# Statistics of two context columns in one VectorE instruction, in a fused decoder kernel

## The chip, the core and the metric

The kernel runs on one core of a Trainium2 chip. The core has TensorE (PE, matmuls; its weight loads are listed apart as PEld), VectorE (DVE), ScalarE (ACT) and GpSimd (POOL), and a queue for data movement, SyncE (SP). Each engine takes its own instructions strictly in their written order and waits, where it must, for semaphores that other engines or transfers raise. The metric is the device time of one execution in microseconds (us).

## The reference, cut to what matters

The input x has 8 sequences of 256 tokens and 1024 features; a second input, ctx, has the same shape. Three blocks follow each other, each added to its own input:

```python
x = x + attn(layernorm(x))                 # 4 layers: recurrence over time, then a 128-512-128 feed-forward
x = x + xattn(layernorm(x), ctx)           # the mask comes from ctx
x = x + ffn(layernorm(x))                  # 8 experts, the best 2 for each token
```

The change concerns the second block. For each sequence and each of the 1024 features (there called L), it takes the 256 tokens (there called channels, C) and keeps the `k = 154` with the largest ctx value:

```python
_, topk_idx = jax.lax.top_k(cm, k)                 # k = 154 of 256
mask = zeros.at[b_idx, l_idx, topk_idx].set(1.0)
crucial_features    = mask * x
subcrucial_features = (1 - mask) * x
# maxima and means of both over the channels -> a 7-tap filter -> two gates per feature
return crucial_features * A_S1 + subcrucial_features * A_S2
```

## The kernel before, in words

*Layout.* Features lie on the 128 partitions. ctx is read as 64 columns, one for each of 8 sequences and 8 groups of 128 features; a column is a 128 x 256 tile whose 256 channels lie side by side in fp32. The columns are worked in `PARTS = 4` batches of `GH = 16`; a batch is one tile `ctx` of 128 x 16 x 256, with two buffers.

*The mask without sorting.* `search(hb)` (L200 to L282) is a generator that handles one batch and yields between its parts. It looks for a threshold in each column:

- The guess (L214 to L228): `bn_stats` of each column, then the spread `sd` (L219, and a power of one half on POOL, L220), then the first trial `trial` (L224) and two ends of a bracket around it (L225, L226).
- Four rounds (L229 to L249): ACT counts with 16 `Sign` instructions with an accumulator (L233) how many channels lie above the trial. DVE compares the counts (L236, L237), moves the ends (L239) and forms the next trial (L243 to L248). ACT's next round needs that trial.
- The tail (L250 to L277): three DVE instructions for each column (L255, L257, L258) find the last few values; L281 then writes the mask. `fails` notes a column whose search didn't end; if any did not, a slow search runs (L717 on).

`bn_stats` on a row of values gives six numbers: count, mean and sum of squared deviations of the values at even places, then the same three of those at odd places. The guess uses only two: the even mean (index 1, L224) and the even sum of squares (index 2, L219).

*What stands around it.* While the four searches go, the kernel runs the first block: 16 cells (4 layers x 4 chunks of 512 tokens). A cell is `recurrence` (L586 to L597: scale to y, two multiplications by the turn table, four scans, all on DVE), `second_norm` (L602 to L611) and `feedforward` (L618 to L626); each normalisation goes over PE (L574), DVE (`ve`, L351), POOL (a power, L352) and PE again (L166). Then come `put_out` (L630 on), `normed_x1` (L325) and `kept_and_dropped` (L315, L318), which sums x under the mask of the same chunk. `advance` mixes the searches' parts between the cells. After that the gates, the routing and the experts' matmuls follow (L1098).

*The start.* `load_rows(c)` (L382 to L393) loads 2 MB of x by rows and takes their statistics on DVE (L387, L388). All four loads use **one** buffer, so the load of rows(c+1) waits for the statistics of rows(c). On SP's queue the transfers stand in this order: win, rows(0), x(0), ctx of batch one, w1, w2, rows(1), x(1), half of x(2), rows(2), the other half of x(2), ctx of batch two, rows(3), x(3), then 18 stores of zeros (L412), wo (L653), and the ctx of batches three and four, which wait for a free ctx buffer. `start(c)` projects x(c) to h (L536, L541). The table `turn` is built in a chain of dependent DVE instructions (L439 to L442 for layer 0). The weights are prepared in between: b2f (L556), PE's 16 small matmuls L561 from w1, b1f (L563) from their result, and the scalings L549, L550, L552 and L565.

*What sets the order.* The kernel isn't written in the order in which it runs. A planner (the Tile framework) takes the program, estimates for each instruction when it could start, and lays down one fixed order for each engine; it also puts in the semaphore waits. So an edit in one place can change the order elsewhere.

Of the kernel before, what the change touches and what calls it, by code (L numbers as in the profile page):

```python
# [13 lines left out]
ALU = mybir.AluOpType  # L14
# [3 lines left out]
B, S, D = 8, 256, 1024  # L18
# [24 lines left out]
TINY = 1e-30  # L43
# [3 lines left out]
GH = B * NK // PARTS  # L47
TRIALS = 5
SHARE = -0.2563
# [18 lines left out]
def decoder_kernel(ctx: ExitStack, tc: tile.TileContext, x_t, x_rows, ctx_t, vecs, win_t, w1_t, w2_t, wout_t,  # L68
# [106 lines left out]
    with ExitStack() as early:  # L175
# [6 lines left out]
        v = nc.vector  # L182
# [11 lines left out]
        def load_ctx(hb):  # L194
            ctx_h = tkp.tile([P, GH, S], F32, tag="ctx", name="ctx", bufs=2)
            for q in range(GH // 4):
                b, g = divmod(hb * (GH // 4) + q, 2)
                nc.sync.dma_start(out=ctx_h[:, 4 * q : 4 * q + 4, :].rearrange("p j c -> p (j c)"),
                                  in_=ctx_t[b, g])
            return ctx_h  # L200
# [3 lines left out]
        def search(hb):  # L204

            ctx_h = ctxs[hb] if hb < len(ctxs) else load_ctx(hb)
            def small(name, n=1, dt=F32):
                shape = [P, GH] if n == 1 else [P, GH, n]
                return tkp.tile(shape, dt, tag=f"tk_{name}", name=f"tk_{name}", bufs=2)

            def pair(name, dt=F32):
                return tkp.tile([P, 2, GH], dt, tag=f"tk_{name}", name=f"tk_{name}", bufs=2)

            st = small("st", 6)  # L214
            for i in range(GH):
                v.bn_stats(st[:, i, :], ctx_h[:, i, :])

            sd = small("sd")
            v.tensor_scalar(sd, st[:, :, 2], 2.0 / S, TINY, ALU.mult, ALU.add)  # L219
            nc.gpsimd.tensor_tensor(sd, sd, power, ALU.pow)  # L220

            trial = pair("trial")
            ends = tkp.tile([P, 2, 2, GH], F32, tag="tk_ends", name="tk_ends", bufs=2)
            v.scalar_tensor_tensor(trial[:, 0], sd, -SHARE, st[:, :, 1], ALU.mult, ALU.subtract)  # L224
            v.scalar_tensor_tensor(ends[:, 0, 0], sd, REACH, trial[:, 0], ALU.mult, ALU.add)  # L225
            v.scalar_tensor_tensor(ends[:, 0, 1], sd, -REACH, trial[:, 0], ALU.mult, ALU.add)  # L226
            nc.gpsimd.memset(ends[:, 1, 0], signs(DROP - REACH * SLOPE))
# [2 lines left out]
            for n in range(TRIALS - 1):  # L230
# [16 lines left out]
                trial = pair("trial")  # L247
                v.tensor_tensor(trial[:, 0], ends[:, 0, 0], w, ALU.subtract)  # L248
                yield  # L249
            t, up, m8 = small("t"), small("up"), small("m8", 8)  # L250
# [32 lines left out]


        waiting = [search(hb) for hb in range(PARTS)]
        going = []
        steps = 0
# [40 lines left out]
        with ExitStack() as dec:  # L328
# [9 lines left out]
            h = [wp.tile([P, CT], F32, tag=f"h{c}", name=f"h{c}") for c in range(NCH)]  # L338
# [80 lines left out]
            v = nc.vector  # L419
# [297 lines left out]
    with tc.If(wrong != 0):  # L717
        with tc.tile_pool(name="slow", bufs=2) as tkp:
            for b in range(B):
                for g in range(2):  # L720
# [3 lines left out]
                    t = tkp.tile([P, 4, S], F32, tag="tk", name="tk")  # L724
# [43 lines left out]
    with tc.tile_pool(name="xattn", bufs=2) as cp:  # L768
# [60 lines left out]
        sd = cp.tile([P, 1], F32, name="bn_sd", bufs=1)  # L829
# [278 lines left out]
    v = nc.vector  # L1108
# [179 lines left out]
```

## Time and profile before

| | |
|---|---|
| Time, median of 3 runs | 1188.22 us (1187.46 to 1188.44) |
| The profiled execution, its own time | 1187.67 us |
| Its span, first to last instruction | 1185.9 us |
| Busy in the span: PE / PEld / DVE / ACT / POOL | 995.7 / 490.5 / 579.8 / 476.3 / 261.8 us |
| `bn_stats` of the search (L216) | 64 of 411 ns, 23.1 us |
| `bn_stats` of the rows (L387) | 32 of 666 ns, 20.3 us |
| `Sign` of the search (L233) with its read of the accumulator | 256 of 504 + 189 ns |
| Last masked sum on DVE (L315) ends | 489.2 us |
| Experts' matmuls (L1098) | 1152 of 597 ns |

The profile is of one execution. A line of the timeline gives the start, the duration, the engine, the line of the kernel, the operation, output <- inputs with their shapes, how many in a row, and in brackets how long the engine stood idle before it and what ended that wait. Busy time on an engine isn't time on the path: instructions on one engine overlap a little, and an engine that waits for another costs only if its lateness is passed on. All line numbers here and below are those of the kernel before; in the changed kernel the lines from L231 on stand 6 further down.

### The profile page before, as it was taken

The page shows a single profiled execution, that of the slowest core. Times are in us where ns is not written, and L with a number is a line of the kernel's source. Part 1 is how long each engine was busy: PE and PEld are TensorE (multiplying, and loading weights), DVE is VectorE, ACT ScalarE, POOL GpSimd, SP SyncE. Part 2 cuts the span into 40 slices and gives each one's busy share as a digit, 9 for nine tenths or more (in the row PEclk, how much of TensorE's full clock was granted, in tenths as well). Part 3 has the DMA queues.
Part 4 walks back from the last instruction along what each step waited for, and adds up shares of the span by engine and source line. Part 5 has one row for each costly group of instructions (what it writes and reads, how often), then busy time and mean ns, then how long its engine had stood idle before and what let it go on. Part 6 is the DMA issues. An engine that isn't in the chain of part 4 may idle for free. (4 is left out here: it accounts for less than half of the span.)

```text
span 1185.9 us, 10180 instructions
## 1 busy us (share of the span) xinstructions
PE 995.7 (84%) x2954; PEld 490.5 (41%) x2954; DVE 579.8 (49%) x1783; ACT 476.3 (40%) x1167; POOL 261.8 (22%) x275
## 2 busy tenths in 40 slices
PE   4848878878888687168849999999999999999994
PEld 2414434434444344033424444444444444444442
DVE  8588888868957978787872111111111111111110
ACT  0577667677764567496311211111111111111110
POOL 1111112121111001104476311113213223131111
PEclk8768889989989877578859999999999999999998
DMA  9594010010000000026637854545557477574622
GB/s 386 203 380 168 0 72 1 15 56 1 1 1 1 0 1 1 13 77 227 210 94 240 264 166 116 156 125 123 161 146 231 119 212 212 138 228 96 177 35 37
DMA packets 53840, 144.99 MB, mean 122 GB/s; under 512 B 5232, under 2 KB 14448, under 8 KB 51984
## 3 DMA queue, kind: packets, MB, share of 16 engines
q0 software_dynamic: 17728, 59.88, 20.3%
q1 hardware_dynamic: 35472, 83.97, 19.6%
q8 instruction: 25, 0.41, 0.1%
q10 hardware_dynamic: 576, 0.41, 0.1%
q14 instruction: 39, 0.32, 0.1%
HBM read 106.61 MB, written 37.64 MB: 122 GB/s over the span
## 5 line engine op out<-in xcount | busy, mean ns | idle before, releaser
L1098 PE MATMUL ps_mm<-w_x,xT 128*128 128x512 f32 x1152 | 505.7, 597 | 2.9 <-ACT xT L1092 0.6
L1098 PEld LDWEIGHTS ps_mm<-w_x,xT 128*128 128x128 f32 x1152 | 216.7, 191 | 270.5 <-issue 259.4
L1101 DVE SCALAR_TENSOR_TENSOR y<-ps_mm,held,y 128x512 f32<-128x512 f32 x56 | 42.0, 751 | 358.6 <-PE ps_mm L1098 358.6
L233 ACT ACTIVATE tkj<-ctx,tk_trial 128x256 f32<-128x256 f32 x256 | 129.1, 504 | 40.8 <-DVE tk_trial L248 22.7
L1084 ACT ACTIVATE y<-src,held 128x1024 f32<-128x1024 f32 x28 | 32.1, 1147 | 195.5 <-DMA out_dram<-y,to 160.2
L1092 ACT COPY xT<-ps_tp 128x512 f32<-128x512 f32 x37 | 21.7, 586 | 189.6 <-PE ps_tp L1090 177.5
L352 POOL TENSOR_TENSOR rs<-ve,minus_half 128x4 f32<-128x4 f32 x36 | 41.1, 1142 | 246.5 <-DVE ve L351 224.2
L618 PE MATMUL ps_tp<-z,w 128*128 128x512 f32 x128 | 69.5, 648 | 13.9 <-DVE z L611 12.9
L1102 POOL DMA_INDIRECT out_dram<-y,to x28 | 44.6, 1592 | 159.2 <-DVE y L1101 117.3
L166 PE MATMUL ps_st<-ident,rs 128*128 128x128 f32 x160 | 29.6, 320 | 57.7 <-POOL rs L352 49.2
L1071 POOL DMA_INDIRECT src<-x_rows,to x28 | 29.0, 1035 | 165.3 <-ACT y L1084 164.1
L1101 DVE SCALAR_TENSOR_TENSOR y<-ps_mm,got,y 128x512 f32<-128x512 f32 x18 | 13.5, 750 | 102.7 <-PE ps_mm L1098 96.0
L318 ACT ACTIVATE comb<-comb 128x256 f32<-128x256 f32 x128 | 51.5, 403 | 27.9 <-DVE smax L315 26.2
L624 PE MATMUL ps_mm<-f,w 128*128 128x512 f32 x128 | 61.7, 602 | 0.0
L166 PEld LDWEIGHTS ps_st<-ident,rs 128*128 128x128 f32 x160 | 20.5, 159 | 83.7 <-POOL rs L352 73.5
L1090 PE MATMUL ps_tp<-ident,xn 128*128 128x128 f32 x296 | 39.9, 278 | 16.4 <-ACT xn L1082 16.4
L621 ACT ACTIVATE f<-ps_tp,b1f 128x512 f32<-128x512 f32 x64 | 43.5, 682 | 23.4 <-PE ps_tp L618 23.1
L1090 PEld LDWEIGHTS ps_tp<-ident,xn 128*128 128x128 f32 x296 | 35.4, 144 | 35.9 <-issue 19.0
L574 PEld LDWEIGHTS ps_cols<-mean_w,sq 128*128 128x128 f32 x288 | 39.5, 202 | 22.8 <-ACT sq L571 11.3
L233 ACT ACTIVATION_READ_ACCUMULATOR tkj<-ctx,tk_trial 128x1 f32 x256 | 48.3, 189 | 0.0
L604 PE MATMUL ps_mm<-mi,turned_w 128*128 128x512 f32 x64 | 38.2, 705 | 8.0 <-DVE mi L597 8.0
L536 PE MATMUL ps_tp<-x,win 128*128 128x512 f32 x64 | 37.1, 735 | 5.9 <-DMA x<-in_x_t_dram 2.8
(371 smaller groups left out, 1434.1 us busy)
## 6 DMA issues: line engine op xcount, KB each, us to landing
w_x<-in_expert_w_dram SPq DMA_DIRECT2D x36, 1024.0 KB, 8.4
out_dram<-zero SPq DMA_DIRECT2D x17, 512.0 KB, 7.7
rows<-in_x_rows_dram SPq DMA_DIRECT2D x4, 2048.0 KB, 8.6
x<-in_x_t_dram SPq DMA_DIRECT2D x8, 1024.0 KB, 12.8
ctx<-in_ctx_t_dram SPq DMA_DIRECT2D x16, 512.0 KB, 9.1
x_rows<-row SPq DMA_DIRECT2D x16, 512.0 KB, 2.8
w<-in_w_t_dram SPq DMA_DIRECT2D x2, 1024.0 KB, 11.6
win<-in_win_t_dram SPq DMA_DIRECT2D x1, 512.0 KB, 3.7
```

Source lines behind the costliest of these rows:

```text
L166: nc.tensor.transpose(rb[:, q * P : (q + 1) * P], rs[:, q : q + 1].to_broadcast([P, P]), ident)
L233: nc.scalar.activation(junk, ctx_h[:, i, :], AF.Sign, bias=trial[:, 0, i : i + 1], accum_out=trial[:, 1, i : i + 1])
L318: nc.scalar.activation(comb[:, st, :], comb[:, st, :], AF.Copy, accum_out=ssum[:, st, b, k : k + 1])
L352: nc.gpsimd.tensor_tensor(out_, ve, root, ALU.pow)
L574: nc.tensor.matmul(out=st[:, q : q + 1], lhsT=sq[:, q * P : (q + 1) * P], rhs=mean_w, start=True, stop=True)
L618: nc.tensor.matmul(out=fps, lhsT=w1[:, l, f * P : (f + 1) * P], rhs=z, start=True, stop=True)
L621: nc.scalar.activation(ft, fps, AF.Silu, bias=b1[:, 4 * l + f : 4 * l + f + 1])
L624: nc.tensor.matmul(out=xc, lhsT=w2[:, l, f, :], rhs=ft, start=False, stop=(f == DFF // P - 1), skip_group_check=True)
L1090: nc.tensor.transpose(tp[:, k * P : (k + 1) * P], xn[:, kk * P : (kk + 1) * P], ident)
L1098: nc.tensor.matmul(out=op, lhsT=xT[:, k * P : (k + 1) * P], rhs=ws[k][g], start=(k == 0), stop=(k == NK - 1))
L1101: nc.vector.scalar_tensor_tensor(y[:, o], op, weight, y[:, o], ALU.mult, ALU.add)
L1102: added = nc.gpsimd.indirect_dma_start(out=out[0:ROWS_THEN, :] if apart else out, out_offset=bass.IndirectOffsetOnAxis(ap=token, axis=0), ...
```

## The change

One `bn_stats` now reads two columns at once. Its input is the even channels of both, and goes through them in turn: channel 0 of the first column, channel 0 of the second, channel 2 of the first, and so on, 256 values. The values at even places are then the first column's even channels, those at odd places the second column's. The six numbers of an instruction are thus count, mean and sum of squares of two columns, and fill the first six of the twelve places of a pair in `st`. The reads of `st` are changed to find them there, and `sd` and `trial` are seen in pairs for that; their values are those of the kernel before. There are 8 such instructions for a batch instead of 16.

```diff
@@ -212,16 +212,22 @@
             st = small("st", 6)
-            for i in range(GH):
-                v.bn_stats(st[:, i, :], ctx_h[:, i, :])
+            for i in range(0, GH, 2):
+
+                v.bn_stats(st[:, i : i + 2, :].rearrange("p c f -> p (c f)")[:, 0:6],
+                           ctx_h[:, i : i + 2, ::2].rearrange("p c s -> p s c"))
+            st = st.rearrange("p (h c) f -> p h (c f)", c=2)[:, :, 0:6].rearrange("p h (c f) -> p h c f", c=2)
+            def halves(t):
+                return t.rearrange("p (h c) -> p h c", c=2)
 
             sd = small("sd")
-            v.tensor_scalar(sd, st[:, :, 2], 2.0 / S, TINY, ALU.mult, ALU.add)
+            v.tensor_scalar(halves(sd), st[:, :, :, 2], 2.0 / S, TINY, ALU.mult, ALU.add)
             nc.gpsimd.tensor_tensor(sd, sd, power, ALU.pow)
 
             trial = pair("trial")
             ends = tkp.tile([P, 2, 2, GH], F32, tag="tk_ends", name="tk_ends", bufs=2)
-            v.scalar_tensor_tensor(trial[:, 0], sd, -SHARE, st[:, :, 1], ALU.mult, ALU.subtract)
+            v.scalar_tensor_tensor(halves(trial[:, 0]), halves(sd), -SHARE, st[:, :, :, 1], ALU.mult,
+                                   ALU.subtract)
```

## The prediction

> **What bounds the kernel now.** I began with the page: its chain of waits covers only the last 1.4% of the span (the last expert's matmuls), so it can't price this change. The stages come from the busy time in stretches (columns after the stretch: its length, busy time of PE, PE's weight loads, DVE, ACT and POOL with instruction counts, granted TensorE clock, DMA share, GB/s).
>
> ```profile
> 0.00:80.00 80.00, 42.30 (x117) 24.77 (x118) 58.28 (x250) 33.24 (x106) 15.16 (x41) 0.77 0.80 316
> 80.00:260.00 180.00, 146.74 (x487) 75.26 (x485) 153.71 (x466) 128.02 (x355) 28.79 (x26) 0.88 0.20 71
> 260.00:425.00 165.00, 138.12 (x447) 71.06 (x448) 128.33 (x396) 103.28 (x290) 18.99 (x17) 0.90 0.00 1
> 525.00:1186.00 661.00, 614.55 (x1743) 291.15 (x1741) 159.18 (x410) 143.91 (x182) 189.87 (x171) 0.96 0.57 161
> ```
>
> From 525 us on PE is the bound and holds nothing of the change. From 80 to 425 us DVE is the busiest engine, 282 of 345 us, and idles 63 us in short waits. From 0 to 80 us it is the loads, but not steadily, as shorter stretches show:
>
> ```profile
> 30.00:35.00 5.00, 1.72 (x6) 0.76 (x4) 2.19 (x13) 1.20 (x5) 3.00 (x3) 1.00 1.01 419
> 40.00:45.00 5.00, 5.00 (x17) 3.85 (x17) 3.83 (x9) 4.49 (x16) 0.00 (x0) 0.50 0.01 3
> 45.00:50.00 5.00, 5.00 (x7) 2.02 (x6) 5.00 (x15) 0.00 (x0) 0.00 (x0) 0.50 0.00 0
> 50.00:55.00 5.00, 5.00 (x12) 2.09 (x12) 1.73 (x12) 2.98 (x10) 1.27 (x1) 0.99 0.83 293
> ```
>
> DMA moves nothing from 40 to 50 us. The cause is in the timeline of DVE:
>
> ```profile
> 33.54 0.19 DVE L224 SCALAR_TENSOR_TENSOR tk_trial<-tk_sd,tk_st 128x16 f32<-128x16 f32 x1 [2.81 <-POOL tk_sd L220]
> ...
> 41.17 0.17 DVE L563 TENSOR_TENSOR b1f<-ps_cols,vec 128x16 f32<-128x16 f32 x1 [3.18 <-PE ps_cols L561]
> ...
> 44.72 1.87 DVE L387 BATCH_NORM_STATS2 bn<-rows 128x6 f32<-128x512 f32 x3
> ...
> 58.05 1.88 DVE L387 BATCH_NORM_STATS2 bn<-rows 128x6 f32<-128x512 f32 x3 [6.26 <-DMA rows<-in_x_rows_dram]
> ...
> 71.75 1.88 DVE L387 BATCH_NORM_STATS2 bn<-rows 128x6 f32<-128x512 f32 x3 [2.17 <-DMA rows<-in_x_rows_dram]
> ...
> 80.64 0.69 DVE L586 TENSOR_TENSOR y<-h,ps_st 128x512 f32<-128x512 f32 x1 [1.80 <-PE ps_st L166]
> ```
>
> and in those of the SP queue and ACT:
>
> ```profile
> 49.79 0.33 SPq L382 DMA_DIRECT2D rows<-in_x_rows_dram  x1
> ...
> 63.14 0.33 SPq L382 DMA_DIRECT2D rows<-in_x_rows_dram  x1
> ```
>
> ```profile
> 51.89 0.51 ACT L233 ACTIVATE tkj<-ctx,tk_trial 128x256 f32<-128x256 f32 x1 [7.18 <-DVE tk_trial L248]
> ...
> 61.80 0.19 ACT L233 ACTIVATION_READ_ACCUMULATOR tkj<-ctx,tk_trial 128x1 f32 x1
> ```
>
> All four row loads use one buffer, so rows(c+1) starts when DVE has ended the statistics (L387) of rows(c): 49.76 lets 49.79 go, 63.11 lets 63.14 go; the later x and context loads queue behind on SP. Rows(2) takes 8.26 us to DVE's next start, rows(3) 8.6. Behind rows(3)'s statistics stands the first `ve` of the recurrence (L351, 77.29), so the first y at 80.64 waits for this loop of DVE and DMA.
>
> **The change, part by part.** *Removed:* 32 of 64 statistics. *Price of the new one:* it reads the same 256 elements, but every element lies 1 KB from the one before, or nearly. The rows:
>
> ```profile
> L216 DVE BATCH_NORM_STATS2 tk_st<-ctx x64: 368/410/428, 22.8 to 245.5; 128x6 f32<-128x256 f32 x64
> ```
>
> Four in a row at 166.92 take 1.40 us and twelve at 241.89 take 4.01: a pitch of 0.334. Nothing in the trace reads 256 strided elements. The nearest row is L224, which reads 16 elements at 24 bytes: 182 ns, against 175 and 169 for L225 and L226, the same form without a stride. 10 ns over 16 elements is 0.6 ns each; times 256, 0.16 us, so **0.57 us, pitch 0.49** (an estimate). Lower end: 0.41, since L219 reads at the same stride in 160 ns, no slower than contiguous L236 (162). Upper end: the cost per element doubled. L387 takes 666 ns for 512 elements and L216 411 for 256, so one element costs 1.0 ns: 0.41 + 0.27 = 0.68, pitch 0.60.
>
> Here two pages of the Trainium skill disagree. "SBUF — State Buffer", section "Door 1: The DMA port swizzle", says that accesses run at full rate only when at least two fall into one 16-byte line; this pattern never gives two in a row, so the rule speaks against the change. "VectorE: DVE Perf Modes", section "Mode 1× (REGULAR) — the baseline", says that fp32 with odd strides still yields a result per cycle. By the first, with the doubled element as my estimate, all 32 pairs save 32 x (0.667 - 0.60) = 2.1 us of DVE; by the second 32 x 0.334 = 10.7; by the row 5.7. L224 lies between, so I keep its value. The reads of the results change only from a stride of 24 bytes to pairs 12 bytes apart on 16 elements (L219, L224): nothing, at most 16 ns four times.
>
> *Batch one, 22.8 us.* Statistics and links of the turn table alternate at 0.467 a pair (16 from 22.81 to 29.82). Now 8 pairs at 0.467 + 0.16 and two small copies moved among them: the last ends at 27.9, the spread (L219) starts at 27.95 instead of 30.31, and 3.23 later (POOL's power, as before) the trial at 31.2. So 2.3 us are won there. But the built order has moved the rest of the links behind the trial: twelve, without statistics between, at 0.28, 0.33 and 0.40 us for 32, 64 and 128 elements (durations 0.21, 0.25, 0.33 plus 0.07 between dependent ones) = 4.05, with 0.45 for what else stands there. **h (L541) comes at 35.7 instead of 33.88**; b2f follows at 36.3, PE's L561 runs from 36.5 to 42.4 (5.9 as before), b1f waits for it: +1.2. Behind it come L550, two L565 and the four L552 (3.4 us), then L236: it waits for ACT's first round, which starts at 31.4 and needs 16 x 0.637 + 1.1 = 11.3, done at 42.7, so no wait. L236, L237, one L565 and two L239 cost 0.7. Rows(1)'s statistics start at 46.6 instead of 44.72 and end 4.9 later; SP sends rows(2) at 51.5, **+1.7**.
>
> *A wait that moves, 62 us.* Before, seven of rows(2)'s eight statistics preceded the L236 of the second round. In the built changed order L236, L237 and both L239 stand **ahead** of all eight, so DVE waits for ACT's round with rows(2) landed. The second trial is ready at 52.5, ACT's round lasts 10.1 (51.89 to 61.99), so 62.8. Queued behind: rows(2)'s statistics, then SP's rows(3), x(3) and the zero stores. The statistics run from 63.2 to 68.25 (5.06 as before); rows(3) goes at 68.25 against 63.14, **+5.1**. Without this wait they would start at 51.5 + 8.3 = 59.8 and the delay stay 1.7. Batch two's 8 removed statistics lie in the wait for rows(3): nothing gained; that wait was 2.17 and now grows. Rows(3), 8.6 later as before, is at DVE at 76.85, and the first y at 85.7. No deadline absorbs that: ACT, PE and DVE all start the recurrence from it, and the later context loads wait for masks that shift too. With statistics at 0.41 the same steps give +3.9, at 0.68 +6.0.
>
> *Batches three and four, 167 and 239 us.* Eight fewer each: 16 x 0.334 - 8 x 0.494 = 1.4 us, 2.8 for both. Batch three stands between waits that would take over (0.80 for DMA, 0.52 and 0.57 for PE), batch four is packed. I count two thirds: **-1.9**; bounds 0 and, with the cheap statistics, -5.3.
>
> *The order from 175 us on* is rewritten on PE, ACT and DVE until about 480: an L586 is put ahead of search steps (1.4 us of them filled its wait before), search four goes a round later against the cells. I can't price it from rows; the likeliest case takes it at 0, and the rivals its two ends.
>
> **Sum:** the profiled execution took 1187.67 us (span 1185.9 and 1.8 around it), 0.5 under the median 1188.22. 1187.67 + 5.1 - 1.9 = 1190.9, carried to the median **1191.4**. With cheap statistics +3.9 - 3.6 gives 1188.5, with doubled ones +6.0 - 0.7 gives 1193.5.
>
> **The rivals.** *The order wins.* Between 80 and 490 us DVE waits 17.5 us for PE at L351 and 14.0 at L586. If the rewritten order fills a third more of these 31.5, 10.5 us come back: 1191.4 - 10.5 = 1181, faster; it decides as soon as it wins over 5.6. For it: in these stages DVE has 13 us less to do in the planner's order. Against: the filler it moves must also keep ACT's rounds going. *The order loses* the same third: 1202. For it: filler was taken from in front of L586. *The stride doubles the element:* 1193.5; for it L224, against it L219. *It doesn't do what it says:* were the guess worse, the slow search would run; but mean and spread of the even channels were the ones used before.
>
> **How the numbers follow.** Likeliest 0.46, its own range 1187.5 to 1195; order wins 0.26 (1177 to 1186); doubled element 0.14 (1191.5 to 1196); order loses 0.12 (1195 to 1205); slow search 0.02. Leaving out about one in ten on each side gives 1182 to 1199. Within 0.2% (1185.8 to 1190.6, about what a measurement tells from no change) lies 0.20, the lower half of the likeliest case; faster 0.28, slower 0.52.
>
> **What would show it.** Right: 32 statistics at 0.5 to 0.6 us; h at 35 to 36.5; SP's third rows at about 51.5 and its fourth at 67 to 69; L236 idle for ACT some 3 us near 60; the first y at 84.5 to 86.7. Wrong: rows(3) leaving before 65, the first y at 81 or earlier, or, with these right, the end of the masked sums (489.2 us before) moved by more than 3 us from +3.

## The result and the profile after

The changed kernel takes 1193.56 us (median of 8 runs, 1191.29 to 1197.81); the kernel before, measured beside it, 1189.82 us (8 runs). The ratio is **1.0037, interval 1.0023 to 1.0051**: slower by 3.7 us between the medians and by 4.4 us (2.7 to 6.1) by the ratio, beyond the 0.2% that a measurement tells. In a second session the ratio was 1.0028 (1.0017 to 1.0040), 3.3 us. The prediction was 1191.4 us, 3.2 over the time given for the kernel before, 1188.22 us, whose median here is itself 1.6 us higher.

The profiled execution took 1194.59 us with a span of 1192.8. VectorE's busy time fell from 579.8 to 569.9 us, so the change saved 9.9 us of work on the engine it touches and the kernel got slower. Busy time in stretches of the changed kernel (columns as in the prediction):

```profile
0.00:80.00 80.00, 41.54 (x114) 24.77 (x114) 52.55 (x216) 31.65 (x100) 12.85 (x39) 0.83 0.74 295
80.00:260.00 180.00, 146.20 (x497) 74.89 (x498) 150.77 (x458) 125.83 (x348) 30.55 (x28) 0.90 0.23 80
260.00:425.00 165.00, 135.39 (x441) 70.45 (x440) 127.75 (x407) 106.24 (x304) 18.69 (x16) 0.90 0.00 1
525.00:1186.00 661.00, 617.52 (x1751) 290.80 (x1749) 162.15 (x413) 146.91 (x188) 190.34 (x171) 0.96 0.57 161
```

In the first 80 us DVE is busy 5.7 us less than before (52.55 for 58.28; a part of its work has only slid past 80 us) and the transfers move less (0.74 of their time busy for 0.80, 295 GB/s for 316): the saved time became a wait. Where it sits is in DVE's timeline of the changed kernel (its lines from L231 on stand 6 further down):

```profile
30.51 0.19 DVE L229 SCALAR_TENSOR_TENSOR tk_trial<-tk_sd,tk_st 128x16 f32<-128x16 f32 x1 [2.90 <-POOL tk_sd L225]
...
34.58 0.68 DVE L547 TENSOR_TENSOR h<-ps_tp,rbs 128x512 f32<-128x512 f32 x1
...
42.21 0.17 DVE L569 TENSOR_TENSOR b1f<-ps_cols,vec 128x16 f32<-128x16 f32 x1 [2.44 <-PE ps_cols L567]
...
46.33 1.87 DVE L393 BATCH_NORM_STATS2 bn<-rows 128x6 f32<-128x512 f32 x3
...
62.64 0.17 DVE L242 TENSOR_SCALAR tk_is_low<-tk_trial 128x16 uint8<-128x16 f32 x1 [10.23 <-ACT tkj L239]
...
63.06 1.87 DVE L393 BATCH_NORM_STATS2 bn<-rows 128x6 f32<-128x512 f32 x3
...
75.90 1.88 DVE L393 BATCH_NORM_STATS2 bn<-rows 128x6 f32<-128x512 f32 x3 [3.76 <-DMA rows<-in_x_rows_dram]
...
84.80 0.69 DVE L592 TENSOR_TENSOR y<-h,ps_st 128x512 f32<-128x512 f32 x1 [1.80 <-PE ps_st L166]
```

The trial comes 3.0 us earlier than before, and everything after it later. The third start of the row statistics no longer waits for a transfer but stands behind L242, which waits for ACT. SP's queue shows what that does to the loads:

```profile
51.41 0.33 SPq L388 DMA_DIRECT2D rows<-in_x_rows_dram  x1
68.14 0.33 SPq L388 DMA_DIRECT2D rows<-in_x_rows_dram  x1
```

They left at 49.79 and 63.14 before: +1.6 and +5.0. The first y is 4.2 us late. Four marks of the profiled executions follow the lateness through the kernel; experiments that stand in the same rows are explained below. "Order before" and "order after" mean the built order up to the masked sums; e4, e6, e7, e8 and e9 add work only behind it.

| us | first y | last (16th) y | last masked sum ends | first expert matmul |
|---|---|---|---|---|
| before | 80.64 | 330.77 | 489.2 | 616.7 |
| order before: e4, e6, e9 | 80.20, 80.21, 82.19 | 330.71, 330.72, 332.50 | 489.2, 490.5, 492.2 | (work added) |
| after | 84.80 | 321.77 | 492.5 | 621.0 |
| order after: again, e7, e8 | 83.93, 83.48, 84.78 | 322.87, 323.27, 324.25 | 493.7, 494.1, 495.1 | 622.4, (work added) |
| e1, last three batches alone | 79.84 | 319.62 | 487.8 | 617.2 |
| e2, first batch alone, twice | 85.06, 84.86 | 336.31, 335.96 | 494.8, 491.7 | 622.4, 618.5 |
| e3, rows first | 80.85 | 318.92 | 487.1 | 615.6 |

The last masked sum comes at 490.3 on average in the four executions of the order before and at 493.9 in the four of the order after: 3.6 us apart, as the medians are. Between, the rewritten order runs the cells 9 us ahead (321.77 for 330.77) and the fourth search 10 us behind (its `fails` at 419.65 for 409.43). These cancel by the masked sums, which need both.

### The profile page after: what moved, and what is told of

Same layout as the page of the kernel before. It is cut to its first block, busy times and chain, and to the rows that moved or that the text cites. A ratio compares the mean times of both kernels' runs of the same rounds, so it can differ in the third digit from the quotient of the medians.

```text
span 1192.8 us, 10147 instructions
## 1 busy us (share of the span) xinstructions
PE 995.7 (83%) x2954; PEld 491.2 (41%) x2954; DVE 569.9 (48%) x1751; ACT 475.1 (40%) x1167; POOL 261.3 (22%) x275
## 5 line engine op out<-in xcount | busy, mean ns | idle before, releaser
L624 PE MATMUL ps_tp<-z,w 128*128 128x512 f32 x128 | 67.0, 627 | 6.6 <-DVE z L617 4.7
L324 ACT ACTIVATE comb<-comb 128x256 f32<-128x256 f32 x128 | 51.5, 403 | 28.3 <-DVE smax L321 28.0
L651 PE MATMUL ps_tp<-zm,wo 128*128 128x512 f32 x64 | 42.0, 795 | 3.5 <-DVE x L652 3.5
```

Source lines behind the costliest of these rows:

```text
L324: nc.scalar.activation(comb[:, st, :], comb[:, st, :], AF.Copy, accum_out=ssum[:, st, b, k : k + 1])
L624: nc.tensor.matmul(out=fps, lhsT=w1[:, l, f * P : (f + 1) * P], rhs=z, start=True, stop=True)
L651: nc.tensor.matmul(out=op, lhsT=wo[:, k, :], rhs=zm, start=True, stop=True)
```

## The experiments

**What was asked.** Theory: the loss is made in the first 80 us, by the late h and above all by the count comparison that moved ahead of the row statistics; the rewritten order later is worth little. Rival: the later order loses, or the stage behind the masked sums, which the change doesn't touch.

**e1: pairs in the last three batches alone.**

```diff
-            for i in range(0, GH, 2):
+            if hb > 0:
                 ...            # the pairs of the changed kernel
+            else:
                 ...            # the single statistics of the kernel before
```

Its built order has the start of the kernel before and the later order of the changed one.

> Batch one keeps its 16 single statistics, batches two to four take pairs. In the built order the start (to 80 us) is then that of the kernel before, with rows(2)'s statistics ahead of the second L236, and everything after about 165 us is that of the changed kernel. Theory (the loss is the moved wait at the start): the first y back at 80.6 us (84.8 in the changed kernel), the whole about 4 us faster than the changed kernel, 0.9985 to 1.0005 of before, end of the masked sums near 488. Rival (the loss comes from the rewritten order after 165 us, where search four ends 10 us later): the first y at 80.6 all the same, but the time stays at about 1.003 of before and the masked sums end at 492 or later.

Measured: 1189.56 us, ratio **1.0002** (0.9988 to 1.0015). The loss is gone when the first batch alone is put back.

**e2: pairs in the first batch alone** (`if hb == 0`), the reverse: the late start, then the later order of the kernel before.

> Only batch one takes pairs. The start is then that of the changed kernel, with L236 ahead of rows(2)'s statistics, and everything after is in the order of the kernel before. Theory (moved wait): the first y at 84.8 us, all later marks 4 us behind those of before, the masked sums end near 493.4, time 1.0030 to 1.0040 of before. Rival (later order): the first y at 84.8, but the lateness is made up in the waits of 80 to 490 us, the masked sums end near 489 and the time is within 0.1% of before.

Measured: 1191.15 us, ratio 1.0013 (0.9998 to 1.0027). First y 4.4 us behind the kernel before, last masked sum 5.6 us behind, so the marks agreed with the theory and the time did less. It was run once more beside the changed kernel:

> Statistics in pairs for the first batch alone, a second time. Last masked sum at 494.8 again (5.6 us behind the kernel before). Theory: its median is 1.003 to 1.006 of before and not below that of the changed kernel; the 1.0013 of the first session was the variation of the last stage. Rival (the last stage takes back part of a delay): 1.0000 to 1.0020 again, at or below the changed kernel.

> The changed kernel once more, for a second profile of it and a comparison with the two below in one session. Theory: the order of each engine is fixed, so the last masked sum comes again at 492.5 within 0.3 us; span less that time differs from the first profile's 700.3 by some us (the kernels so far had 696.7 to 700.3 in a stage that is the same for all), and the median is 1.0025 to 1.0050 of before. Rival (the 3.6 us behind the masked sums belong to the change): span less last masked sum is again 700 or more.

Measured: e2 1.0025 (1.0011 to 1.0039), the changed kernel 1.0028 (1.0017 to 1.0040). So the first batch alone slows the kernel; against the changed kernel beside it (1192.54 for e2's 1191.57), the other three batches make no difference that shows. e2's 1.0025 is under the theory's 1.003 and over the rival's 1.0020. The theory also said that e2 would not come out below the changed kernel, and its median is 1.0 us below; 11 and 9 runs can't tell that from nothing. Its last masked sum came at 491.7 this time, with the same order: one profile places this mark to about 3 us, no better. The changed kernel's came at 493.7, not within the expected 0.3 of 492.5. Span less last masked sum was 698.6 in place of 700.3, under the 700 or more that the rival asked for, with 696.7 in the kernel before; so the rival that put 3.6 us of loss behind the masked sums isn't borne out.

**e3: the row statistics first.** The changed kernel, with the count comparisons of the first search's first two rounds made to wait for the row statistics that stood ahead of them before:

```diff
-                v.tensor_scalar(is_low, trial[:, 1], signs(DROP), None, ALU.is_gt)
+                low = v.tensor_scalar(is_low, trial[:, 1], signs(DROP), None, ALU.is_gt).ins
+                if hb == 0 and n < 2:
+                    after(low, [rows_read[n + 1]], "rows first")
...
-                        nc.vector.bn_stats(st[:, g, :], r[:, q, g * CT : (g + 1) * CT])
+                        rows_read[c] = nc.vector.bn_stats(st[:, g, :], r[:, q, g * CT : (g + 1) * CT]).ins
```

> All four batches take pairs as in the changed kernel; the L236 of rounds one and two of the first search are tied behind the statistics of rows(1) and rows(2), so the wait for ACT at 52 to 62 us no longer stands ahead of rows(2)'s statistics. The later order is that of the changed kernel. Theory: DVE's first 10.2 us wait falls to about 6 (for rows(2)), SP's fourth rows leaves at 64 to 65 instead of 68.1, the first y at 81 to 82 instead of 84.8, time about 3 us under the changed kernel, 1.000 to 1.002 of before. Rival: no change from the changed kernel's 1.0037.

Measured: 1190.91 us, ratio 1.0010 (0.9998 to 1.0023). DVE's timeline of e3:

```profile
34.59 0.68 DVE L550 TENSOR_TENSOR h<-ps_tp,rbs 128x512 f32<-128x512 f32 x1
...
45.13 1.87 DVE L396 BATCH_NORM_STATS2 bn<-rows 128x6 f32<-128x512 f32 x3
...
58.48 1.88 DVE L396 BATCH_NORM_STATS2 bn<-rows 128x6 f32<-128x512 f32 x3 [6.54 <-DMA rows<-in_x_rows_dram]
...
64.04 0.12 DVE L242 TENSOR_SCALAR tk_is_low<-tk_trial 128x16 uint8<-128x16 f32 x1
...
80.85 0.69 DVE L595 TENSOR_TENSOR y<-h,ps_st 128x512 f32<-128x512 f32 x1 [1.80 <-PE ps_st L166]
```

h is as late as in the changed kernel (34.59), and still the row statistics start within 0.5 us of the kernel before (45.13 for 44.72, 58.48 for 58.05), wait for their transfer again, and the first y is back at 80.85.

Not all of the difference is the order's. b1f waits for PE's small matmuls L561 (L567 in the changed kernel, L570 in e3), and the row statistics stand behind b1f. In turn the kernel before, the changed kernel, e3, and the second execution of the changed kernel:

```profile
35.25 5.88 PE L561 MATMUL ps_cols<-vec,w 128*128 128x1 f32 x32 [3.53 <-DVE b2f L556]
```

```profile
35.39 6.79 PE L567 MATMUL ps_cols<-vec,w 128*128 128x1 f32 x32 [4.09 <-DVE b2f L562]
```

```profile
35.40 5.75 PE L570 MATMUL ps_cols<-vec,w 128*128 128x1 f32 x32 [3.53 <-DVE b2f L565]
```

```profile
35.45 5.75 PE L567 MATMUL ps_cols<-vec,w 128*128 128x1 f32 x32 [3.52 <-DVE b2f L562]
```

The late h moves their start by 0.2 us or less. Their length follows the granted clock (last section), and the changed kernel had 6.79 in one execution and 5.75 in another. From their end to the first y it takes 39.1 to 40.5 us in the seven executions in which the rows are first (before, e1, e3, e4, e5, e6, e9; mean 39.7) and 42.4 to 42.7 in the six others (mean 42.6). So of the 4.2 us the places of L242 in the queue cost about 3, the late h some 0.1, and the clock in that one execution 0.9.

The ratio fell from 1.0037 to 1.0010, the better part of the loss, but the two intervals touch, and between the medians 2.0 us are left (1188.95 for the kernel before). The trace shows the cause of the late start, and the time agrees with it without proving its whole size.

**e4: what the read pattern costs.** The kernel before with 48 `bn_stats` of 256 elements on a tile of ones, eight of each pattern, in the section that prepares the token lists:

```diff
+    flat = probe.rearrange("p c s -> p (c s)")
+    pairs = probe[:, 0:2, :].rearrange("p c s -> p s c")
+    ...                                        # each eight times:
+        v.bn_stats(heard[:, 0, i, :], flat[:, 0:S])
+        v.bn_stats(heard[:, 1, i, :], flat[:, 0 : 2 * S : 2])
+        v.bn_stats(heard[:, 2, i, :], flat[:, 0 : 4 * S : 4])
+        v.bn_stats(heard[:, 3, i, :], probe[:, 0:2, 0:P])
+        v.bn_stats(heard[:, 4, i, :], pairs[:, 0:P, :])
+        v.bn_stats(heard[:, 5, i, :], pairs[:, ::2, :])
```

> The kernel before with 48 statistics of 256 elements added late, where DVE is mostly idle, 8 of each read pattern: in a row; every second element (8 bytes apart); every fourth (16 bytes); one column's 128 and then the next one's; two columns in turn without leaving out a channel; two columns in turn, even channels only (the changed kernel's pattern). Theory (a read costs more when it begins a new 16-byte line): in a row and one column after the other 0.41 us, every second element 0.41, every fourth and both patterns in turn 0.47. Rival (the two-element inner loop costs): every fourth 0.41, both in turn 0.47. Time within 1 us of before.

Measured, the group by tile (min/median/max in ns), in the order of the diff:

```profile
L1203 DVE BATCH_NORM_STATS2 heard<-probe x8: 377/420/424, 592.8 to 613.1; 128x6 f32<-128x256 f32 x8
L1205 DVE BATCH_NORM_STATS2 heard<-probe x8: 407/416/421, 614.8 to 641.3; 128x6 f32<-128x256 f32 x8
L1207 DVE BATCH_NORM_STATS2 heard<-probe x8: 597/598/601, 641.7 to 645.3; 128x6 f32<-128x256 f32 x8
L1209 DVE BATCH_NORM_STATS2 heard<-probe x8: 407/408/415, 645.8 to 649.3; 128x6 f32<-128x256 f32 x8
L1211 DVE BATCH_NORM_STATS2 heard<-probe x8: 407/410/414, 649.7 to 652.0; 128x6 f32<-128x256 f32 x8
L1213 DVE BATCH_NORM_STATS2 heard<-probe x8: 462/464/466, 652.3 to 655.0; 128x6 f32<-128x256 f32 x8
```

Neither theory fits. A stride of 8 bytes is free, and so is going through two columns in turn when all channels are taken (0.410). One column at 16 bytes costs 0.18 us more; two columns in turn at 8 bytes each, the change's pattern, 0.05 more. The run's single time, 1201.21 us, is 12 over the kernel before: the probes lay ahead of the first expert matmul (631.3 for 616.7), against what was expected of them.

**e5: e3 with the pattern that e4 found free.** The pairs take channels 0 to 127 of both columns in place of the even ones, so the guess rests on other samples:

```diff
-                           ctx_h[:, i : i + 2, ::2].rearrange("p c s -> p s c"))
+                           ctx_h[:, i : i + 2, 0:P].rearrange("p c s -> p s c"))
```

> The changed kernel with two edits: the first search's rounds two and three wait behind the statistics of the next rows, so that the moved wait is gone, and the pairs take the first 128 channels of each column in turn in place of the even ones (0.410 us each[...]). The statistics are of other channels, so the guess is another one, of the same count of samples. Theory: eight instructions of batch one 0.4 us shorter, last masked sum at 486.5 to 487.2, median 0.9975 to 0.9995 of before. Rival (the cost is in the later order alone): last masked sum at 492 and a median of 1.003.

Measured: **2025.04 us**, ratio 1.7014. The statistics took what e4 said, but the search failed somewhere, and the slow search ran (groups of e5, by tile and by line):

```profile
L217 DVE BATCH_NORM_STATS2 tk_st<-ctx x32: 369/418/433, 22.8 to 246.9; 128x6 f32<-128x256 f32 x32
```

```profile
L740 DVE MAX8 m<-tk 128x8 f32<-128x256 f32 x832 | 348.8, 425 | 28.9 <-ACT tk L734 6.5
L743 DVE MATCH_REPLACE8 tk<-m,tk 128x256 f32<-128x256 f32 x832 | 338.9, 408 | 0.0
```

Worked out with the search's formulas on the reference's inputs, 2 of the 8192 columns (64 tiles x 128 partitions) end with their threshold outside the eight values that the tail looks at; with the even channels none does. That costs 836 us. Of the two expectations the times can't be read from this run, but the last masked sum ahead of the slow search can:

```profile
491.46 0.08 DVE L323 DVE_READ_ACCUMULATOR2_ANT smax<- 128x1 f32 x1
```

The theory said 486.5 to 487.2 and missed; the rival's 492 is nearer, although the first y came early (81.45). It doesn't speak for the rival: e1 and e3 have the same later order and had 487.8 and 487.1, and one profile places this mark to about 3 us.

**e6: a pure delay behind the masked sums.** The kernel before with twelve dependent multiplications by 1.0:

```diff
+        for _ in range(12):
+            nc.vector.tensor_scalar(z, z, 1.0, None, ALU.mult)
         half = cp.tile([P, P], F32, name="half", bufs=1)
```

> The kernel before with twelve multiplications of zc by 1.0 (128x128, each reading the result of the one ahead of it) put after the convolution and before its mean: a stretch in which VectorE is alone on the path, 7 us behind the last masked sum, so every one counts. By the kernel's own multiplication of that tile (L834, 0.28 us, next step 0.3 us later) the chain is 3.5 to 4.0 us. The last masked sum stays at 489.2. Theory (a delay ahead of the last stage reaches the end whole): first expert matmul 3.5 to 4 us later, median 1.003 of before. Rival (the last stage, in which TensorE is the bound and its clock varies, takes back part of a delay): first expert matmul later by the same, median at most 1.0013.

Measured: 1191.25 us, ratio 1.0017 (1.0008 to 1.0026), 2.0 us (1.0 to 3.1). The chain took less than expected, on DVE's timeline:

```profile
502.81 3.10 DVE L812 TENSOR_SCALAR zc<-zc 128x128 f32<-128x128 f32 x12
```

By the profile the first expert matmul came 4.6 us late (621.3), 3.1 from the chain and 1.3 from the last masked sum, at 490.5 and not at 489.2 as expected. The time is between the theory's 1.003 and the rival's 1.0013, and the top of its interval is just the 3.1 us: most of the delay arrives, but that all of it does isn't shown.

**e7, e8, e9: the router's first matmuls.** In the kernels so far with the order before (and e2) the router's first sixteen matmuls (L870, `gwc`) had taken 8.3 to 8.6 us, in those with the later order of the change 9.8 to 10.0. Was that a cost of the order? The same delay was put into the changed kernel, twelve and six multiplications, and six into the kernel before.

> The changed kernel with the twelve multiplications of zc by 1.0 behind the convolution (3.1 us in the run on the kernel before). The question is the router's first group of sixteen matmuls (gwc): 8.3 to 8.6 us in the kernels with the later order of the kernel before, 9.8 to 10.0 in those with that of the change, where the granted clock rises from 0.5 to 1.0 some 3 us later after the group's start. Theory (the later order sets it): 9.8 to 10.0 again. Rival (it is where the group falls in the clock's own steps, so a delay moves it): another value, 8.5 or one between.

> The same with six multiplications, half the delay (1.6 us). Theory (the later order sets it): the router's first group 9.8 to 10.0 us. Rival (the clock's own steps): a value that differs from that of the run with twelve by more than 0.3 us.

> The kernel before with six multiplications. Theory (the later order sets it): the router's first group 8.3 to 8.6 us, last masked sum at 489.2 to 490.5. Rival (the clock's own steps): 9 us or more in this or in one of the two runs on the changed kernel 9 us or less.

Measured: 8.43, 9.19 and 9.40 us (times of the one run each: 1195.58, 1195.95 and 1193.79; one of the kernel before beside them, 1186.55). PE's timeline of e7, e8 and e9 in turn:

```profile
525.98 8.43 PE L878 MATMUL ps_st<-x,gwc 128*8 128x512 f32 x16 [1.43 <-DVE x L1011]
```

```profile
525.40 9.19 PE L878 MATMUL ps_st<-x,gwc 128*8 128x512 f32 x16 [1.43 <-DVE x L1011]
```

```profile
522.50 9.40 PE L872 MATMUL ps_st<-x,gwc 128*8 128x512 f32 x16 [1.43 <-DVE x L1005]
```

The rival stands: the same order gives 8.43 or 9.98, by where the group falls in the steps of the clock. That order and duration had agreed in nine executions was chance, or a matter of when each got there. It is not a cost of the change.

## Why the prediction was right, and where its terms were off

*The price of the statistic.* Predicted 0.57 us with a pitch of 0.49, ends 0.41 and 0.68. Measured on the changed kernel:

```profile
L217 DVE BATCH_NORM_STATS2 tk_st<-ctx x32: 461/473/492, 22.8 to 248.1; 128x6 f32<-128x256 f32 x32
```

and 2.02 us for five in a row, a pitch of 0.39. So it lies inside the ends, a quarter of the way from the cheap one, and the row taken (L224) overstated it. Neither page of the Trainium skill that was weighed there has it right for this case. "SBUF — State Buffer" ("Door 1: The DMA port swizzle") would have made the alternation between columns slow, and e4 measured it free; 8 bytes free and 16 bytes slow within one column agree with it. "VectorE: DVE Perf Modes" ("Mode 1× (REGULAR) — the baseline"), as the prediction took it, would have made all strides free, and 16 bytes cost 0.18 us in 256 elements.

*Batch one.* Trial predicted at 31.2, measured 30.51; h 35.7 and 34.58. The moved turn links took their place behind the trial as read from the order; the cheaper statistics brought the trial forward by 0.7 us, and the links took 4.1 us where 4.5 were counted. Rows(1)'s statistics 46.6 and 46.33; rows(2) leaves at 51.5 and 51.41. That they agree is in part luck. The +1.2 that b1f was to lose by the late h was not there: L561 was to start at 36.5 and started at 35.39, 0.14 later than before. It took 6.79 us where 5.9 was carried over, so it ended at 42.18 for 42.4. In the second execution it took 5.75, the statistics started at 45.36, and rows(2) left at 50.44. What the order itself adds was right: from b1f to the statistics 4.1 us were counted, and they took 4.12, for 3.55 before.

*The moved wait.* ACT's round predicted to end at 62.8 and the row statistics to run from 63.2 to 68.25; measured 62.64 and 63.06, and rows(3) left at 68.14, +5.0. This step carried the prediction, and e3 confirmed it by taking the cause away. One reading in it was wrong: L242 stood idle for 10.23 us, not "some 3 us". DVE had nothing else to do from 52.4; only the last 3 us or so of the wait fell after the rows had landed (an estimate: 51.41 and the 8.26 us of before).

*The first y.* Predicted +5.1, measured +4.2, or +3.4 between the means of four executions each (84.25 and 80.81). The term at fault in the first execution is the flight of rows(3), 7.76 us from its issue to DVE's start where 8.6 was carried over. Counted from the end of L561, free of its clock, the order is worth 3.0 (42.6 and 39.7).

*Batches three and four, -1.9, and the later order, 0.* e1, which has exactly these two, came out at 1.0002, 0.2 us with an interval from -1.4 to +1.8; in one session the changed kernel took 1192.54 and e2, which has neither, 1191.57. So the two together are near 0, and the -1.9 was not there to be had, or the later order took it back; these can't be told apart, since the planner changed the later order with the statistics of these batches. That the sum was good is in part luck: its two terms erred against each other, +3.0 to 4.2 for +5.1, and about 0 for -1.9.

*The rivals.* "The order wins" named two waits, 31.5 us together, as its source. Waits of DVE between 80 and 490 us in the changed kernel (total, times, longest):

```profile
DVE ve L357 <- PE ps_cols L580: 16.0, 17, 2.4
DVE y L592 <- PE ps_st L166: 14.5, 14, 2.9
...
DVE ve L357 <- PE ps_cols L373: 6.4, 2, 5.9
```

They are 30.5 us now, where a third was to go, and a new one of 5.9 us has come at L357: the filler was moved, not found. DVE's busy time from 80 to 425 us fell by 3.5 us (278.5 for 282.0), where the planner's order had 13 less. "The order loses" is out by e1. "The stride doubles the element" is out by 0.473 us. The slow search did not run in the changed kernel; e5 shows how near a different sample of the channels can come to it, so 0.02 was its chance only because the samples stayed the same.

*What was to show it.* The third and fourth row loads (51.41, 68.14), the first y (84.80) and the masked sums (+3.3 in the profile, +3.6 in the means, where +3 was said) were inside what was said. In the other executions of this order the first y was 83.93, 83.48 and 84.78, twice short of the 84.5 that was said. h at 34.58 was below its 35 to 36.5, and the statistic at 0.473 below its 0.5 to 0.6.

*Slips without weight in the sum.* From 80 to 425 us the busiest engine is PE, by the prediction's own rows (284.9 us for DVE's 282.0). Before, all eight of rows(2)'s statistics stood ahead of L236 (the last at 62.47, L236 at 63.03), not seven. The 0.28 for faster holds the slow search's 0.02, which would be slower.

## What to carry to other kernels

Work that is taken off an engine early in a program is worth what waits behind it, and a planner may hand its place to an instruction that waits: after an edit, list for each load what stands ahead of the instruction that frees its buffer, in the order as built. Here 9.9 us less work on VectorE moved one comparison ahead of the row statistics, and the transfer behind them left 5 us late. Where only a sample's place is changed to suit an access pattern, price the fallback too: e5 saved 0.05 us on each statistic and paid 836.

## What the runs showed of the hardware that was not expected

**The clock of TensorE moves single stages by over a microsecond.** Granted clock (third column from the end) in stretches of 2 us, first of the kernel before, then of the changed one:

```profile
518.00:520.00 2.00, 1.90 (x3) 0.38 (x4) 2.00 (x3) 2.00 (x6) 0.00 (x0) 0.50 0.00 0
520.00:522.00 2.00, 2.00 (x4) 0.32 (x3) 2.00 (x3) 2.00 (x6) 0.00 (x0) 0.70 0.00 0
522.00:524.00 2.00, 2.00 (x6) 0.45 (x5) 2.00 (x3) 2.00 (x6) 0.00 (x0) 1.00 0.00 0
```

```profile
522.00:524.00 2.00, 2.00 (x4) 0.41 (x3) 2.00 (x3) 2.00 (x5) 0.00 (x0) 0.50 0.00 0
524.00:526.00 2.00, 2.00 (x3) 0.28 (x2) 2.00 (x3) 2.00 (x5) 0.00 (x0) 0.50 0.00 0
526.00:528.00 2.00, 2.00 (x4) 0.34 (x3) 2.00 (x3) 2.00 (x5) 0.00 (x0) 0.71 0.00 0
```

The router's group starts at 518.10 and 521.20. In stretches of 0.1 us the clock goes from 0.50 to 1.00 at 521.18 in the kernel before, 3.1 us after that, and at 527.16 in the changed one, 6.0 us after, and the group takes 8.55 and 9.98 us: 2.9 us more at half the clock, 1.4 us longer. With a delay ahead (e7, e8, e9) it took 8.43, 9.19 and 9.40, with the step 2.8, 4.4 and 4.8 us after its start. The small matmuls L561 at 35 us show the same the other way round: 5.04 us in e1, where the clock fell from 1.00 to 0.50 2.2 us after their start, and 6.99 in e2, where it fell ahead of it.

The steps lie on a grid. In the kernel before the first ones come at 16.01, 26.25, 36.49, 50.14, 60.38 and 63.80 us, which are 3, 3, 4, 3 and 1 times 3.41 us apart. The grid's place differs between executions of one kernel: the drop near 36 us came at 35.64 and 36.84 in the two of the changed kernel. So the same work meets a step sooner or later without any change of order. Why the clock rises at one point of the grid and not at the one before was not tested.

The last masked sum, too, moved by up to 3.1 us between executions of one order (e2: 494.8 and 491.7). A mark from one profile is good to some 3 us here, so a change of this size needs its median, or several profiles, or a mark counted from the end of the group that the clock moves.

**A stride of 16 bytes costs, one of 8 does not.** 256 fp32 elements in `bn_stats`: 0.420 us in a row, 0.416 at 8 bytes, 0.598 at 16 bytes (0.7 ns more for each element), 0.410 from two columns 1 KB apart in turn, 0.464 from these at 8 bytes each.
